# Where layer 1 of a graph network splits x into bf16 parts, and what its first product pass multiplies with

## The chip, the cores and the metric

One core of a Trainium2 chip runs the whole kernel in one launch. The metric is device microseconds of that core, first instruction to last; the median of several runs is quoted, and one execution was recorded by the hardware profiler. The core has five engines that run side by side: TensorE (PE in the profile; its weight loads are PEld), VectorE (DVE), ScalarE (ACT), GpSimd (POOL), and SyncE (SP), which here only issues DMA transfers.

## What is computed

Two SAGE layers on a graph of 12,500 nodes, 200,000 edges and 256 features, a dense layer, the residual and a layer norm. The reference, cut to its core:

```python
def _sage_conv(x, src, dst, W_l, b_l, W_r):
    msgs = x[src]
    agg = jax.ops.segment_sum(msgs, dst, num_segments=N_NODES)
    deg = jax.ops.segment_sum(jnp.ones((src.shape[0],), x.dtype), dst, num_segments=N_NODES)
    mean = agg / jnp.maximum(deg, 1.0)[:, None]
    return mean @ W_l + b_l + x @ W_r
...
h = jax.nn.relu(_sage_conv(x, src, dst, W1_l, b1, W1_r))
h = jax.nn.relu(_sage_conv(h, src, dst, W2_l, b2, W2_r))
return h @ W3 + b3
...
x = _layernorm(x + _L0_gnn_ref(x, edge_index, ...), axis=-1)
```

The edges come sorted by `dst`, and `dst` is 12500·u² of a uniform u, so that low nodes have very many edges.

## The kernel before

Nodes lie in blocks of 128 (98 blocks, the last one short). Each layer aggregates in two ways.

**Rounds (the cold nodes).** Nodes from 1536 up, in layer 1, get their neighbours by gathers. A round is four indirect DMAs on POOL (`gathered`, L266, issue on L273), each of 128 rows of 1 KB of x, into one of four `got` buffers; PE sums the rows by small products (`part_ps`, L285), ACT copies the sums out (L295), PE spreads them over nodes (`sum_ps`, L301, L307), and DVE adds them to a ring (L311, L315). Layer 1 has 257 rounds, layer 2 has 235. Finished blocks of nodes then go through `first_block` (L1055): x is loaded and transposed, PE multiplies with the weights (L1024, L1031), and h is written out as fp32 (L1075) and, split in three bf16 parts by `parts` (L689), as `h3_d` (L1078).

**Count products (the hot nodes).** The first 1536 nodes in layer 1 come in six groups of 256, taken in the order 5, 4, 3, 2, 1, 0. For a group, `count` (L803) builds a matrix of how many edges lead from each source node to each of the group's nodes: DVE makes comparisons (`pick` L821, `low` L824, `aft` L829), PE multiplies them (L859, L863), and ACT copies the counts into the bf16 matrix `counts` (L865). There are four `pick` buffers (L611). Then `product` (L725) multiplies x, block by block, with that matrix into `dense_ps`; `degrees` (L877) sums its columns.

A count is exact in bf16, but x is not: x is the exact sum of three bf16 parts (upper half of the fp32 bits, upper half of the rest, and what is then left). So a block's product is either 2 fp32 matmuls of 128x256 (the *plain* form, L765), for which ACT first widens the bf16 counts of two blocks to fp32 (`wide`, L762), or 6 bf16 matmuls of 128x256 on the three parts (L750), read back from `x3_d` in DRAM (L747, two blocks in one load of 384 KB). Which block takes which form stands in `stages_1` (L938):

- pass 1 (group 5): all 98 blocks plain; blocks 0 to 47 are also split here (`parts`: two DVE subtractions L694, L695 and two ACT copies L696, L697 for each block, 128x256) and written to `x3_d` (L771, 192 KB a block);
- pass 2 (group 4): blocks 0 to 47 from `x3_d`, blocks 48 to 97 plain, and split here;
- passes 3 to 6: all blocks from `x3_d`.

The split goes into three buffers `split3` (L600), which `first_block` uses for h too. x comes in pairs of blocks into the four `rows` buffers (L732, L736), three pairs ahead; `wide` has two buffers.

**What sets the order.** PE and POOL run in the order in which the program is written; the order on the others is made by the compiler from it. `layer` (L621) writes that order: before each round it spends a budget, `room_for` (5.3 for layer 1, L1119), in planned us for each of PE, DVE and ACT, with costs written out by hand (`ROUND`, `GROUP`, `DEGREE`, `COST_*` on L892 and L893, `count_cost`): first the round's own cost, then pieces of `first_block`, then *filler* until the fullest engine has its budget. The filler is `stages_1`: while one group is counted, the product of the group counted before is interleaved with it (`mixed`, L901), with the store of its counts (`stored`, L913) for layer 2. In the last 8 rounds whatever is left of the filler goes out at once. `freed` (L706) makes a load wait for the first gather product after those products that last used the buffer. SP issues all loads and stores but the gathers, in its order, each waiting in the queue for its data or its buffer.

Of the kernel before, what the change touches and what calls it, by code (L numbers as in the profile page):

```python
# [8 lines left out]
F32 = mybir.dt.float32  # L9
F32R = mybir.dt.float32r  # L10
F16 = mybir.dt.float16
BF16 = mybir.dt.bfloat16
# [3 lines left out]
OP = mybir.AluOpType  # L16
# [9 lines left out]
P = 128  # L26
# [23 lines left out]
def by_runs(  # L50
# [27 lines left out]
    nc = tc.nc  # L78
    N, D = x.shape
    E = src.shape[0]  # L80
    NB = -(-N // P)
    NC = D // P
# [23 lines left out]
    HG1, HG, DN = 6, 8, 256  # L106
# [7 lines left out]
    WIDEST = max(ROOMS)  # L114
# [18 lines left out]
    x3_d = dram.tile([P, NB, 3, D], BF16, name="x3_d")  # L133
# [183 lines left out]
    with tc.tile_pool(name="setup", bufs=1) as su, \  # L317
# [32 lines left out]
        whole = (NT // G) * G  # L350
        with nc.allow_non_contiguous_dma(reason="one edge of each tile"):
# [5 lines left out]
            if NT > whole:  # L357
                left = NT - whole
# [56 lines left out]
        first = su.tile([P, CH], F32, name="first")  # L415
# [55 lines left out]
        gathers_1 = Gathers(x, False)  # L471
# [20 lines left out]
        start = su.tile([P, HC], F32, name="start")  # L492
# [11 lines left out]
        for g in ORDER:  # L504
            c0, c1 = spans[g]
            n = c1 - c0
# [10 lines left out]
            of = off_f[:, lows[g]:highs[g]]  # L517
# [20 lines left out]
        for sign in (-1, 1):  # L538
            law = su.tile([1, NG], F32, name="law", bufs=2)
            for since, by in SLACKS:  # L540
                c = -(-since // G)
# [13 lines left out]
        for t in range(0, HT, 32):  # L555
            n = min(32, HT - t)
# [40 lines left out]
    keep = ctx.enter_context(tc.tile_pool(name="keep", bufs=1))  # L597

    SPLIT = 3
    split3 = keep.tile([P, SPLIT, 3, D], BF16, name="split")  # L600
# [3 lines left out]
    def held(g):  # L604

        return counts[ORDER.index(g) % 2]
# [1 line left out]
    NEAR = int(at_most(FIRST)) + room(FIRST - 1)  # L608
    assert NEAR <= DN

    picks = [keep.tile([P, WIDEST * NB], BF16, name=f"pick{i}") for i in range(4)]  # L611

    work = ctx.enter_context(tc.tile_pool(name="work", bufs=2))
    dense_pool = ctx.enter_context(tc.tile_pool(name="dense_ps", bufs=1, space=PSUM))
# [74 lines left out]
    def parts(t, s, rest):  # L689

        def upper(a):
            return a.bitcast(BF16).rearrange("p (n h) -> p n h", h=2)[:, :, 1]

        leaves = nc.vector.tensor_tensor(rest, t, upper(t), op=OP.subtract)  # L694
        nc.vector.tensor_tensor(s[:, 2], rest, upper(rest), op=OP.subtract)  # L695
        nc.scalar.copy(s[:, 0], upper(t))  # L696
        nc.scalar.copy(s[:, 1], upper(rest))  # L697
        return leaves
# [7 lines left out]
    def freed(load, n):  # L706

        if len(used) >= n and used[-n] < len(strips):
            tc.add_manual_dep(load.ins, strips[used[-n]], LANDED, reason="products done")

    N1 = 4
# [10 lines left out]
            freed(nc.sync.dma_start(counted, count_d[:, b:b + 2, pair:pair + 2]), STREAMS)  # L722
        return rows, counted

    def product(g, c_sb, plain=range(0), made=range(0)):  # L725


        ps = dense_pool.tile([P, NC, DN], F32, name="dense_ps")
        nc.tensor.matmul(ps, lhsT=zeros_b, rhs=c_sb[:, :NC, :DN], start=True, stop=False)
        own, wide = {}, {}  # L730

        def x_rows(u):  # L732
            t = rows_pool.tile([P, 2, 3, D], BF16, name="rows", bufs=N1)
            t = t.rearrange("p b k d -> p (b k d)").bitcast(F32)[:, :2 * D].rearrange("p (b d) -> p b d", d=D)
            n = min(2, (N - u * P) // P)
            freed(nc.sync.dma_start(t[:, :n], x[u * P:(u + n) * P].rearrange("(b p) f -> p b f", p=P)), 1)  # L736
            if n < 2:
                left = N - (u + n) * P
                nc.vector.memset(t[:, n], 0.0)
                nc.sync.dma_start(t[:left, n], x[(u + n) * P:N])  # L740
            return t

        for b in range(NB):
            if b not in plain:
                if b % 2 == 0:
                    rows = rows_pool.tile([P, 2, 3, D], BF16, name="rows", bufs=N1)
                    freed(nc.sync.dma_start(rows, x3_d[:, b:b + 2]), N1)  # L747
                for k in range(3):
                    for c in range(NC):
                        nc.tensor.matmul(ps[:, c], lhsT=rows[:, b % 2, k, c * P:(c + 1) * P],  # L750
                                         rhs=c_sb[:, b, :DN], start=False,
                                         stop=b == NB - 1 and k == 2 and c == NC - 1)
                cost = COST_1
            else:
                if b % 2 == 0:
                    for u in range(b, min(b + 2 * N1 - 2, plain[-1]), 2):
                        if u not in own:
                            own[u] = x_rows(u)
                    for u in range(b, min(b + 4, plain[-1]), 2):
                        if u not in wide:  # L760
                            wide[u] = rows_pool.tile([P, 2, DN], F32, name="wide", bufs=2)
                            nc.scalar.copy(wide[u], c_sb[:, u:u + 2, :DN])  # L762
                t, of = own[b - b % 2][:, b % 2], wide[b - b % 2]
                for c in range(NC):
                    nc.tensor.matmul(ps[:, c], lhsT=t[:, c * P:(c + 1) * P], rhs=of[:, b % 2],  # L765
                                     start=False, stop=b == NB - 1 and c == NC - 1)
                cost = COST_FIRST
                if b in made:
                    s = split3[:, b % SPLIT]
                    parts(t, s, work.tile([P, D], F32, name="rest", tag="own", bufs=3))  # L770
                    nc.sync.dma_start(x3_d[:, b], s)  # L771
                    cost = tuple(i + j for i, j in zip(cost, COST_SPLIT))
            if b % 2:
                used.append(len(strips))
            yield cost
        d_sb = rows_pool.tile([P, NC, DN], F32, name="d_sb", bufs=1)
        nc.scalar.copy(d_sb, ps)
        yield g, d_sb
# [98 lines left out]
    def degrees(g, c_sb):  # L877

        n0 = g * (DN // P)
        ps = dense_pool.tile([P, NC, DN], F32, name="dense_ps")  # L880
        for j in range(DN // P):
            for b in range(NB):
                nc.tensor.matmul(ps[:, 0, j:j + 1], lhsT=c_sb[:, b, j * P:(j + 1) * P], rhs=ones_b,
                                 start=b == 0, stop=b == NB - 1)
                if b % 14 == 13:
                    yield COST_DEGREES
        deg = work.tile([P, DN // P], F32, name="d_deg", bufs=1)
        nc.vector.tensor_scalar(deg, ps[:, 0, :DN // P], 1.0, None, op0=OP.max)
        nc.vector.reciprocal(rdeg[:, n0:n0 + DN // P], deg)


    COST_FIRST, COST_1, COST_2 = (0.92, 0.0, 0.31), (0.68, 0.0, 0.0), (0.7, 0.0, 0.0)  # L892
    COST_DEGREES, COST_SPLIT, COST_REST = (0.4, 0.0, 0.0), (0.0, 0.71, 0.81), (0.0, 0.0, 0.3)  # L893

    def count_cost(t):
        n = room(t) * NB
# [21 lines left out]
    def dense(waiting, made, with_deg=None):  # L918
        ready = []
        for p in made:  # L920
            if isinstance(p[0], float):
                yield p
            else:
                ready.append(p)
        if with_deg is not None:
            yield from degrees(with_deg, held(with_deg))
        for g, d_sb in ready:
            for j in range(DN // P):
                waiting.append((g * (DN // P) + j, d_sb[:, :, j * P:(j + 1) * P]))
# [4 lines left out]
    def counting(*gs):  # L934
        whole = sum(max(count_cost(t)) for g in gs for t in range(lows[g], highs[g]))
        return whole + NB // 14 * max(COST_REST) * len(gs)

    def stages_1(waiting):  # L938

        some = NB // 4 * 2  # L940
        for k, (g, last) in enumerate(zip(ORDER[:HG1] + [None], [None] + ORDER)):
            parts = [(count(g, held(g)), counting(g))] if g is not None else []
            if last is not None:
                plain = [range(0), range(NB), range(some, NB)][k] if k < 3 else range(0)
                made = [range(0), range(some), range(some, NB)][k] if k < 3 else range(0)
                whole = 5.0 + sum(max(COST_FIRST[e] * (b in plain) + COST_SPLIT[e] * (b in made) +
                                      COST_1[e] * (b not in plain) for e in range(3)) for b in range(NB))
                parts.append((dense(waiting, product(last, held(last), plain, made), last), whole))
                if last in SAVED:
                    parts.append((stored(last), MOVED))  # L950
            yield parts
# [25 lines left out]
    def staged(stages):  # L977
        def run(waiting):
            for parts in stages(waiting):
                yield from mixed(*parts)  # L980
        return run
# [134 lines left out]
    block_pool = None  # L1116
    with tc.tile_pool(name="count_ps", bufs=2, space=PSUM) as count_pool, \
            tc.tile_pool(name="rows_1", bufs=1) as rows_pool:
        layer(gathers_1, first_block, 3, staged(stages_1), 5.3, 8)  # L1119
    block_pool = ctx.enter_context(tc.tile_pool(name="block_ps", bufs=1, space=PSUM))  # L1120
    beside_pool = ctx.enter_context(tc.tile_pool(name="beside_ps", bufs=1, space=PSUM))
    count_pool = ctx.enter_context(tc.tile_pool(name="count_ps", bufs=1, space=PSUM))
    rows_pool = ctx.enter_context(tc.tile_pool(name="rows_2", bufs=1))
# [384 lines left out]
```

## Time and profile before

| | |
|---|---|
| median of 3 runs | 2687.47 us (2685.69 to 2693.3) |
| the profiled execution | 2681.34 us, its span 2679.5 us |
| mean granted PE clock in it | 0.968 of full speed |
| counting of group 5 ends, pass 1 begins | 181.7 us |
| passes 1 to 6 with their degrees end, about | 391.5, 599.5, 773.8, 960.8, 1252.9, 1401 us |
| last gather of layer 1, first of layer 2 | 1424.8, 1453.6 us |

Times are from the start of the span. Busy time is the time in which an engine ran an instruction; matmuls overlap one another, and their ends are modelled, so that a PE shown as busy is not PE at its peak. "PEclk" is the share of its full clock that TensorE was granted; "DMA share" is the mean busy share of the core's 16 DMA engines. In rows of groups, the numbers behind the bar are busy us and mean ns of one; then the engine's idle time just before them, and who ended it.

### The profile page before, as it was taken

To read this page: it belongs to the slowest core of one execution; us is meant where nothing else is said; L and a number is where in the kernel's file an instruction comes from. 1 tells how busy PE (TensorE), PEld (TensorE's weight loads), DVE (VectorE), ACT (ScalarE), POOL (GpSimd) and SP (SyncE) were. 2 spreads that over 40 slices of the span, in tenths; PEclk is the share of its full clock that TensorE was granted. 3 is DMA by queue.
4 is the path that set the end of the run, shared out by engine and by line. 5 is a ranking of instruction groups with operands and counts; after the bars stand their busy time and mean duration, and the time that the engine had idled before them with its cause. 6 is when DMAs were issued, how large, how long until landed. Compare 5 with 4: busy or idle time off the path is not lost. (4 is left out here: it accounts for less than half of the span.)

```text
span 2679.5 us, 51726 instructions
## 1 busy us (share of the span) xinstructions
PE 2411.8 (90%) x17119; PEld 1506.1 (56%) x17119; DVE 1558.3 (58%) x5514; ACT 1201.1 (45%) x2409; POOL 1910.2 (71%) x1978
## 2 busy tenths in 40 slices
PE   3678999889999999999997999999999999899986
PEld 2245676556776766666674445545455555555555
DVE  6777654775667789987334123544455554544455
ACT  0587764875667752386223012343434443222223
POOL 6767776776777777776664777777777777777772
PEclk8699999989999999999998999999999999999999
DMA  5359779889898777775875777778777777677653
GB/s 136 106 167 310 240 223 304 257 256 298 261 300 277 242 221 217 221 210 169 266 241 170 224 224 230 241 244 251 237 226 242 250 236 218 195 206 212 201 172 95
DMA packets 360737, 602.57 MB, mean 225 GB/s; under 512 B 56093, under 2 KB 244239, under 8 KB 360463
## 3 DMA queue, kind: packets, MB, share of 16 engines
q1 hardware_dynamic: 261637, 340.29, 39.8%
q0 software_dynamic: 94464, 258.08, 32.2%
q8 instruction: 141, 2.31, 0.4%
q10 hardware_dynamic: 4362, 0.80, 0.2%
q14 instruction: 133, 1.09, 0.1%
HBM read 509.09 MB, written 89.87 MB: 224 GB/s over the span
## 5 line engine op out<-in xcount | busy, mean ns | idle before, releaser
L273 POOL DMA_INDIRECT got<-in_x_dram,src_t x1028 | 1010.6, 983 | 412.3 <-issue 256.1
L273 POOL DMA_INDIRECT got<-h_d,src_t x940 | 897.3, 955 | 313.9 <-issue 251.4
L865 ACT CAST counts<-count_ps 128x882 f32 (+3 forms) x688 | 620.4, 902 | 232.7 <-PE count_ps L859 185.0
L859 PE MATMUL count_ps<-pick,low 128*128 128x490 bf16 (+2 forms) x1188 | 350.8, 350 | 56.9 <-ACT counts L865 44.9
L750 PE MATMUL dense_ps<-counts,rows 128*128 128x256 bf16 x2640 | 359.3, 276 | 23.3 <-DMA rows<-x_d 22.5
L285 PE MATMUL part_ps<-got,one 128*32 128x257 f32 (+1 forms) x3936 | 325.3, 403 | 58.7 <-DMA got<-h_d,src_t 34.8
L790 PEld LDWEIGHTS <-rows 128*128 128x128 bf16 x2352 | 214.0, 97 | 259.4 <-issue 81.4
L821 DVE TENSOR_SCALAR pick<-steps,tables 128x686 bf16<-128x686 f16 (+3 forms) x816 | 335.1, 411 | 24.7 <-PE count_ps L863 11.7
L295 ACT COPY some<-part_ps 128x257 f32<-128x257 f32 (+1 forms) x349 | 130.0, 373 | 472.5 <-PE part_ps L285 467.4
L750 PEld LDWEIGHTS <-rows 128*128 128x128 bf16 x2640 | 241.7, 98 | 104.8 <-issue 33.2
L229 DVE TENSOR_TENSOR one<-lo_t,lane_b 128x128 f32<-128x128 bf16 x492 | 140.7, 287 | 233.5 <-PE part_ps L285 232.3
L824 DVE TENSOR_SCALAR low<-lanes,low_t 128x130 bf16<-128x130 f16 x816 | 220.8, 272 | 82.5 <-PE count_ps L863 78.3
L315 DVE TENSOR_TENSOR sums<-sums,sum_ps 128x256 f32 x349 | 143.0, 410 | 154.6 <-PE sum_ps L301 134.8
L301 PE MATMUL sum_ps<-two,some 128*128 128x128 f32 x1396 | 222.6, 283 | 9.7 <-ACT own_t L997 7.6
L301 PEld LDWEIGHTS sum_ps<-two,some 128*128 128x128 f32 x1396 | 202.7, 195 | 41.4 <-ACT own_t L997 12.9
L790 PE MATMUL beside_ps<-counts,rows 128*128 128x512 bf16 x588 | 224.5, 382 | 0.5 <-ACT split L800 0.5
L790 PE MATMUL dense_ps<-counts,rows 128*128 128x512 bf16 x588 | 224.6, 382 | 0.0
L1038 DVE TENSOR_TENSOR own<-block_ps,biases 128x256 f32<-128x256 f32 x196 | 83.0, 424 | 216.9 <-PE block_ps L1031 214.5
L859 PEld LDWEIGHTS <-low 128*128 128x128 bf16 x1188 | 114.7, 99 | 150.4 <-issue 38.2
L285 PEld LDWEIGHTS part_ps<-got,one 128*32 128x32 f32 x3936 | 80.2, 109 | 202.5 <-issue 162.0
L997 ACT COPY own_t<-block_ps 128x256 f32<-128x256 f32 x294 | 105.4, 373 | 168.0 <-PE block_ps L995 164.8
L1034 ACT COPY sums<-zero 128x256 f32<-128x256 f32 x168 | 67.7, 403 | 240.9 <-PE block_ps L1031 240.9
(197 smaller groups left out, 3588.2 us busy)
## 6 DMA issues: line engine op xcount, KB each, us to landing
rows<-x_d SPq DMA_DIRECT2D x220, 384.0 KB
rows<-h_d SPq DMA_DIRECT2D x196, 384.0 KB
count_d<-counts SPq DMA_DIRECT2D x28, 896.0 KB
x_sb<-in_x_dram SPq DMA_DIRECT2D x194, 128.0 KB
h_d<-split SPq DMA_DIRECT2D x98, 192.0 KB
x_d<-split SPq DMA_DIRECT2D x98, 192.0 KB
rows<-in_x_dram SPq DMA_DIRECT2D x72, 256.0 KB
got<-in_x_dram,src_t POOLq DMA_INDIRECT x1028
```

What stands on the lines that cost most here:

```text
L229: nc.vector.tensor_tensor(one, lo[:, a:a + n * (G - 1) + 1:n].unsqueeze(2).to_broadcast([P, G, W]), lane_b[:, :W].unsqueeze(1).to_broadcas ...
L273: rows = nc.gpsimd.indirect_dma_start(out=g[:, j, :D], out_offset=None, in_=self.table, in_offset=bass.IndirectOffsetOnAxis(ap=src_t[:, e: ...
L285: strip = nc.tensor.matmul(part_ps[j * W:(j + 1) * W, :width], lhsT=one[:, j], rhs=g[:, j, :width], start=r == 0, stop=r == n - 1)
L295: nc.scalar.copy(some[:, :width], part_ps[:, :width])
L301: nc.tensor.matmul(sum_ps[:, c], lhsT=some[:, c * P:(c + 1) * P], rhs=two, start=True, stop=True)
L315: adds.append(nc.vector.tensor_add(own, own, sum_ps[:, :NC]).ins)
L750: nc.tensor.matmul(ps[:, c], lhsT=rows[:, b % 2, k, c * P:(c + 1) * P], rhs=c_sb[:, b, :DN], start=False, stop=b == NB - 1 and k == 2 and ...
L790: nc.tensor.matmul(ps[c], lhsT=rows[:, b % 2, k, c * P:(c + 1) * P], rhs=counted[:, b % 2], start=b + k == 0, stop=b == NB - 1 and k == 2)
L821: nc.vector.tensor_scalar(r[:, :w * NB], steps[:, :w * NB], key_t[g][:, t - lo_g:t - lo_g + 1], None, op0=OP.is_equal)
L824: nc.vector.tensor_scalar(low.rearrange("p (a b) -> p a b", a=5), lanes_5[:, :, :LW // 5], low_t[:, t:t + 1], None, op0=OP.is_equal)
L859: nc.tensor.matmul(c[:, a * NB:b * NB], lhsT=s, rhs=r[:, a * NB:b * NB], start=True, stop=alone)
L865: nc.scalar.copy(to[:, :, bass.ds(off_act.at(t), w)], c.rearrange("p (d s) -> p s d", s=NB))
```

## The change

Pass 1 now splits all 98 blocks and multiplies the parts at once; passes 2 to 6 all read `x3_d`. x comes in pairs into two tiles of its own, `x_pair`; `parts_of` splits a pair (128x512) with two subtractions on DVE and two copies on ACT straight into a `rows` tile, which pass 1's bf16 products read and which one store of 384 KB writes to `x3_d`. Loads of x are asked for two pairs ahead and splits one pair ahead. The fp32 products, the widened counts and the use of `split3` for x are gone, and there are three `pick` buffers for four (in both layers). The planned cost of a pass-1 block is 0.68 on PE, 0.61 on DVE and 0.70 on ACT, and layer 1's budget for a round is 5.05 for 5.3. Layer 2's text is otherwise the same.

```diff
-    picks = [keep.tile([P, WIDEST * NB], BF16, name=f"pick{i}") for i in range(4)]
+    picks = [keep.tile([P, WIDEST * NB], BF16, name=f"pick{i}") for i in range(3)]
...
+    def parts_of(t, s):
+        def upper(a):
+            return a.bitcast(BF16).rearrange("p b (n h) -> p b n h", h=2)[:, :, :, 1]
+        rest = rows_pool.tile([P, 2, D], F32, name="rest_2", bufs=1)
+        nc.vector.tensor_tensor(rest, t, upper(t), op=OP.subtract)
+        freed(nc.vector.tensor_tensor(s[:, :, 2], rest, upper(rest), op=OP.subtract), N1)
+        freed(nc.scalar.copy(s[:, :, 0], upper(t)), N1)
+        nc.scalar.copy(s[:, :, 1], upper(rest))
+
+    def x_rows(u):
+        t = rows_pool.tile([P, 2, D], F32, name="x_pair", bufs=2)
+        n = min(2, (N - u * P) // P)
+        nc.sync.dma_start(t[:, :n], x[u * P:(u + n) * P].rearrange("(b p) f -> p b f", p=P))
...
+    def product(g, c_sb, first=False):
         ps = dense_pool.tile([P, NC, DN], F32, name="dense_ps")
         nc.tensor.matmul(ps, lhsT=zeros_b, rhs=c_sb[:, :NC, :DN], start=True, stop=False)
+        raw, made = {}, {}
         for b in range(NB):
+            if b % 2 == 0 and first:
+                for u in range(b, min(b + 6, NB), 2):
+                    if u not in raw:
+                        raw[u] = x_rows(u)
+                for u in range(b, min(b + 4, NB), 2):
+                    if u not in made:
+                        made[u] = rows_pool.tile([P, 2, 3, D], BF16, name="rows", bufs=N1)
+                        parts_of(raw[u], made[u])
+                        nc.sync.dma_start(x3_d[:, u:u + 2], made[u])
+                rows = made[b]
+            elif b % 2 == 0:
+                rows = rows_pool.tile([P, 2, 3, D], BF16, name="rows", bufs=N1)
+                freed(nc.sync.dma_start(rows, x3_d[:, b:b + 2]), N1)
+            for k in range(3):
                 for c in range(NC):
+                    nc.tensor.matmul(ps[:, c], lhsT=rows[:, b % 2, k, c * P:(c + 1) * P],
+                                     rhs=c_sb[:, b, :DN], start=False,
+                                     stop=b == NB - 1 and k == 2 and c == NC - 1)
...
+            yield COST_FIRST if first else COST_1
...
-    COST_FIRST, COST_1, COST_2 = (0.92, 0.0, 0.31), (0.68, 0.0, 0.0), (0.7, 0.0, 0.0)
-    COST_DEGREES, COST_SPLIT, COST_REST = (0.4, 0.0, 0.0), (0.0, 0.71, 0.81), (0.0, 0.0, 0.3)
+    COST_FIRST, COST_1, COST_2 = (0.68, 0.61, 0.7), (0.68, 0.0, 0.0), (0.7, 0.0, 0.0)
+    COST_DEGREES, COST_REST = (0.4, 0.0, 0.0), (0.0, 0.0, 0.3)
...
-        layer(gathers_1, first_block, 3, staged(stages_1), 5.3, 8)
+        layer(gathers_1, first_block, 3, staged(stages_1), 5.05, 8)
```

More of the change, by code (lines that the diff above doesn't have):

```diff
@@ L723, in loaded @@
         return rows, counted
-    def product(g, c_sb, plain=range(0), made=range(0)):
+    def parts_of(t, s):
[6 more added lines that the diff above has]
+        nc.scalar.copy(s[:, :, 1], upper(rest))
@@ L728, in product @@
+    def x_rows(u):
+        t = rows_pool.tile([P, 2, D], F32, name="x_pair", bufs=2)
+        n = min(2, (N - u * P) // P)
+        nc.sync.dma_start(t[:, :n], x[u * P:(u + n) * P].rearrange("(b p) f -> p b f", p=P))
+        if n < 2:
+            left = N - (u + n) * P
+            nc.vector.memset(t[:, n], 0.0)
+            nc.sync.dma_start(t[:left, n], x[(u + n) * P:N])
+        return t
+    def product(g, c_sb, first=False):
         ps = dense_pool.tile([P, NC, DN], F32, name="dense_ps")
@@ L729, in product @@
         nc.tensor.matmul(ps, lhsT=zeros_b, rhs=c_sb[:, :NC, :DN], start=True, stop=False)
[L730 to L741, printed above, removed]
@@ L743, in product @@
-        for b in range(NB):
[L744 to L763, printed above, removed]
-                for c in range(NC):
[L765 to L772, printed above, removed]
@@ L773, in product @@
             if b % 2:
                 used.append(len(strips))
-            yield cost
+            yield COST_FIRST if first else COST_1
         d_sb = rows_pool.tile([P, NC, DN], F32, name="d_sb", bufs=1)
@@ L938, in stages_1 @@
     def stages_1(waiting):
-        some = NB // 4 * 2
         for k, (g, last) in enumerate(zip(ORDER[:HG1] + [None], [None] + ORDER)):
@@ L943, in stages_1 @@
             if last is not None:
[L944 to L948, printed above, removed]
+                whole = 5.0 + NB * max(COST_FIRST if k == 1 else COST_1)
+                parts.append((dense(waiting, product(last, held(last), k == 1), last), whole))
                 if last in SAVED:
```

## The prediction

> **What bounds the kernel now.** I read the groups first, then the windows of the six passes, then who waits. The edit is in layer 1, which is a race between PE and POOL's gathers.
>
> ```profile
> L273 POOL DMA_INDIRECT got<-in_x_dram,src_t x1028 | 1010.6, 983 | 412.3 <-issue 256.1 <-PE part_ps L285 119.0 <-DMA got<-in_x_dram,src_t 10.9
> ...
> L821 DVE TENSOR_SCALAR pick<-steps,tables 128x686 bf16<-128x686 f16 (+3 forms) x816 | 335.1, 411 | 24.7 <-PE count_ps L863 11.7 <-PE count_ps L859 9.7 <-PE count_ps L848 0.9
> ```
>
> Layer 1's 1028 gathers take 1010.6 us on POOL, and 256.1 us pass between them without a wait: (1010.6+256.1)/1028 = 1.232 us each, 4.93 us for a round of four. That is POOL's floor. Of the rest 119.0 us are waits for PE. (L821 makes the picks; I use it below.)
>
> Windows cut where each pass ends (count behind POOL: gathers issued):
>
> ```profile
> 181.70:391.50 209.80, 192.84 (x1339) 131.69 (x1339) 135.70 (x492) 152.75 (x298) 153.14 (x156) 0.97 0.84 261
> 391.50:599.50 208.00, 185.11 (x1443) 125.60 (x1440) 137.21 (x504) 136.46 (x294) 146.46 (x147) 0.93 0.86 272
> 599.50:773.80 174.30, 168.62 (x1537) 120.09 (x1535) 111.88 (x428) 109.99 (x179) 121.30 (x127) 0.95 0.85 278
> 773.80:960.80 187.00, 181.40 (x1632) 129.14 (x1631) 137.78 (x552) 131.68 (x235) 134.03 (x139) 0.99 0.84 269
> 960.80:1252.90 292.10, 276.39 (x2204) 184.52 (x2205) 265.95 (x992) 151.24 (x319) 213.28 (x220) 0.98 0.69 205
> 1252.90:1401.00 148.10, 139.90 (x1276) 103.93 (x1276) 56.54 (x193) 40.68 (x111) 97.08 (x103) 0.98 0.79 255
> sum 1219.30, PE 1144.26 PEld 794.97 DVE 845.07 ACT 722.80 POOL 865.29; mean PE 190.71 PEld 132.50 DVE 140.84 ACT 120.47 POOL 144.21
> ```
>
> The gathers give 39, 37, 32, 35, 55 and 26 rounds, 223 in all: 1219.3/223 = 5.47 us a round, above POOL's floor and above the planned 5.3. PE is busy in 1144.26 of 1219.30 us and idle in 75.0. So PE sets most of the pace, with POOL 10% behind it. Passes 1 and 2, which the change touches, have 17.0 and 22.9 us of idle PE; pass 3, already pure bf16, has 5.7.
>
> **The change, part by part.**
>
> *fp32 products out, bf16 products in.* The timeline of PE, one block in each form, with the next instruction behind it:
>
> ```profile
> 242.02 1.13 PE L765 MATMUL dense_ps<-wide,rows 128*128 128x256 f32 x4
> 242.99 0.37 PE L859 MATMUL count_ps<-pick,low 128*128 128x490 bf16 x1
> ```
> ```profile
> 399.82 0.61 PE L301 MATMUL sum_ps<-two,some 128*128 128x128 f32 x4
> ...
> 400.51 0.38 PE L859 MATMUL count_ps<-pick,low 128*128 128x490 bf16 x1
> ...
> 401.60 0.64 PE L285 MATMUL part_ps<-got,one 128*32 128x257 f32 x8
> 402.17 0.83 PE L750 MATMUL dense_ps<-counts,rows 128*128 128x256 bf16 x6
> 402.84 0.37 PE L859 MATMUL count_ps<-pick,low 128*128 128x490 bf16 x1
> ```
>
> From start to start a plain block takes 0.97 us (2 matmuls, 4 instructions in the trace), a bf16 block 0.67. The difference is 0.30 us. Plain blocks are 98 in pass 1 and 50 in pass 2: 148 x 0.30 = **44.4 us** less PE work, 29.4 and 15.0.
>
> *ACT and DVE.*
>
> ```profile
> L765 PE MATMUL dense_ps<-wide,rows 128*128 128x256 f32 x592 | 160.2, 396 | 5.6 <-ACT wide L762 5.6
> L229 DVE TENSOR_TENSOR one<-lo_t,lane_b 128x128 f32<-128x128 bf16 x492 | 140.7, 287 | 233.5 <-PE part_ps L285 232.3
> L695 DVE TENSOR_TENSOR split<-rest 128x256 bf16<-128x256 f32 x196 | 80.6, 416 | 38.0 <-DMA x_d<-split 33.9 <-DMA h_d<-split 3.4
> L762 ACT CAST wide<-counts 128x512 f32<-128x512 bf16 x74 | 45.6, 618 | 0.2 <-PE dense_ps L765 0.2
> L694 DVE TENSOR_TENSOR rest<-rows 128x256 f32<-128x256 f32 x98 | 40.0, 416 | 6.3 <-DMA h_d<-own 3.4 <-ACT split L697 2.7
> L696 ACT COPY split<-rows 128x256 bf16<-128x256 bf16 x98 | 39.6, 405 | 37.2 <-DMA x_d<-split 28.5 <-DMA h_d<-split 4.3 <-issue 2.9
> ```
>
> The 592 instructions are the 148 plain blocks. A 128x512 subtraction isn't in the trace. From 287 ns at 128 wide and 416 at 256 it goes on to 416+258 = 674; twice 416 = 832 is the upper end. I take 0.67. A copy at 512 is between 0.41 and 0.81 (one and two of 405); the widening, also 512 wide, took 0.618, which I take. DVE in pass 1: 48 blocks x 0.832 = 39.9 out, 49 pairs x 2 x 0.67 = 65.7 in, so 135.7 becomes about 161. ACT in pass 1: 49 widenings (30.3) and 48 x 0.81 (38.9) out, 60.6 in: about 144. In pass 2 50 blocks x 0.832 (DVE), 50 x 0.81 and 25 x 0.618 (ACT) go, and nothing comes: 41.6 and 56.0 us. None of this is on the path as a sum; it counts by the waits:
>
> ```profile
> PE count_ps L859 <- ACT counts L865: 9.4, 10, 2.8
> PE dense_ps L750 <- DMA rows<-x_d: 5.9, 3, 3.1
> PE dense_ps L883 <- ACT d_sb L777: 5.4, 1, 5.4
> ```
>
> These are PE's longest waits in pass 2. Two are for an ACT that falls from 136 to 80 us of work there. Pass 3 has no such wait in its list. I count **10 us** won of 14.8; the load stays late. In pass 1 PE's waits for `wide` (5.6 us in the L765 row) and ACT's and DVE's for the stores out of three `split3` buffers (28.5 and 33.9, both stages) go. Parts take their place as what PE waits for: a chain of two where there was one copy. I call that even.
>
> *The plan.* Budget and costs are in the code; adding them up as `layer` does gives 39, 36, 32, 34, 55, 26 rounds to the passes before (the trace agrees to a round) and 35, 31, 33, 37, 59, 26 after. The total hardly moves, and each round's own PE work goes with it. So PE's total simply falls by 44.4. But pass 1 now has little PE work: 192.8-29.4-4x1.2 = 158.6 us (1.2: a round's strips, from 401.60 to 402.17, and its spreading, from 399.82 to 400.51, rounded down since not every round spreads). POOL's floor there is 35 x 4.93 = 172.6. With its own waits for PE (13.7 us before), pass 1 takes 186 us, with 27 us of idle PE against 17: **10.4 us** of the saving are lost. Pass 5 has 59 rounds, floor 291; with 281 of PE work and the old 16 idle it takes 297, so POOL doesn't decide there.
>
> *DMA.* Pass 1 moved this:
>
> ```profile
> DMA packets 45462, 54.80 MB, mean 261 GB/s; under 512 B 4590, under 2 KB 40026, under 8 KB 45439
> ```
> ```profile
> 200.00:220.00 20.00, 16.75 (x104) 10.32 (x103) 14.30 (x55) 14.38 (x32) 14.98 (x16) 0.91 1.09 368
> 420.00:440.00 20.00, 14.86 (x99) 9.17 (x97) 5.86 (x22) 6.08 (x10) 7.82 (x9) 0.74 0.87 288
> ```
>
> The stores of 50 more blocks add 9.8 MB, four rounds fewer take 2.1: 62.5 MB. At the 368 GB/s of the fullest window that is 170 us, at pass 1's own ratio (261 GB/s at share 0.84, so 311) 201. The first hides behind 186, the second doesn't; I take 186, since the present split phase ran at 368, and keep 15 us for the range. SP issues 49 fewer stores and 25 more loads of `x3_d`.
>
> *Three picks.* A `pick` waits for the product two steps back instead of three. The 816 picks of both layers now wait 24.7 us in all (the L821 row), nearly all on PE's products. One buffer fewer can't gain; if the waits double and half of that passes on to PE, it costs 12 us. I take 3, near the low end, since a DVE that waits for PE holds nothing up unless DVE is full, as in pass 5 only (265.95 of 292.10).
>
> *Sum:* -44.4 -10 +10.4 +3 = **-41 us**. Layer 2 keeps its text (but for the picks) and its time. The profiled execution took 2681.34, so 2640; the median of the runs was 6.1 higher, so **2646**.
>
> **The rivals.**
>
> *POOL paces (R1).* PE's busy time overlaps its own pipeline. [...] In the rows: POOL's 119.0 us of waits for PE over layer 1 are 119.0/257 = 0.46 us a round, so in the 66 rounds that passes 1 and 2 keep 30 us could be won at most; less the 10.4 of new idle time that is 20, or 2667. The step of 0.67 against 0.97 us speaks for my forecast. For this one speaks a window late in pass 1, where PE shows no idle time at all and POOL still issues 17 gathers in 20 us, its full pace:
>
> ```profile
> 340.00:360.00 20.00, 20.00 (x126) 13.92 (x125) 10.55 (x40) 13.64 (x23) 15.13 (x17) 1.00 0.61 180
> ```
>
> *The floor is reached (R2).* If rounds get as near to their 5.05 as pass 5's came to 5.3, 221 rounds x 5.07 = 1120 instead of 1219; less the 223 x 0.17 = 38 us by which rounds now exceed their 5.3, about 60 us won: 2628.
>
> *Pass 1 starves on x (R3, slower).* x has two tiles, and SP issues a pair's load behind the store of the pair two before, which waits for its parts. So a pair takes (load + split)/2. Pass 1 lasts 49 x that, plus 10 for degrees. How long a load takes when the queues are full:
>
> ```profile
> 417.58 0.45 SPq L747 DMA_DIRECT2D rows<-x_d  x1
> ```
> ```profile
> 419.55 0.82 PE L750 MATMUL dense_ps<-counts,rows 128*128 128x256 bf16 x6
> ...
> 423.52 0.83 PE L750 MATMUL dense_ps<-counts,rows 128*128 128x256 bf16 x6 [3.15 <-DMA rows<-x_d]
> ...
> 425.52 1.49 PE L750 MATMUL dense_ps<-counts,rows 128*128 128x256 bf16 x6
> ```
>
> 5.9 us for 384 KB. With 256 KB at 5 and a split of 2 us the pair takes 3.5: no harm. With a load of 7, behind a 384 KB store in the same queue, and a split of 3.5, it is 5.25: pass 1 lasts 267 us, 81 more than forecast, and the time is 2727. The kernel is slower from 4.5 us a pair on (10+49x4.5 = 231, 45 over the forecast). PE's clock adds to it: after the 3.15 us stall six matmuls took 1.49 us for 0.83, at a granted 0.74. [...] Against the rival: DVE and ACT have room in pass 1, and POOL hides the first 172 us.
>
> *Nothing (R4):* the saving goes into new waits for parts; 2687.
>
> **How the numbers follow.** Forecast 45%, with its own range 2630 to 2662; R1 18%, R2 14%, R3 16%, R4 7%. A measurement tells about 0.3% (8 us) from no change. Faster: forecast, R1 and R2, 0.77; the same 0.07; slower 0.16. The range takes in R1, R2, R4 and the 15 and 12 us of the open prices, and leaves out most of R3 and the lowest end of R2: 2610 to 2700.
>
> **What would show it.** Right: pass 1 near 186 us, pass 2 near 170, passes 3 to 6 within 10 of before; no fp32 rows in `dense_ps`; pairs split in 0.67 and 0.62 us; POOL's waits for PE down to some 80 us. Wrong: PE waiting for `rows` with x loads behind it in pass 1 and a clock under 0.9 (R3); POOL at 1.24 us a gather all through with PE idle (R1); DVE waiting for L859 at the picks in pass 5 (their price). What I can't see is the order that the compiler gives DVE, ACT and SP for the new text.

## The result, and the profile after

The kernel after takes **2660.14 us** (median of 4 runs, 2652.59 to 2667.07), the kernel before 2686.58 on the same chip: a ratio of 0.9897 (95% 0.9864 to 0.993), 26 us faster where 41 were forecast, and inside the forecast's own range of 2630 to 2662. The profiled execution is the slowest of the four: 2667.07 us, with a span of 2665.2.

The windows of the six passes, in the columns of the prediction's table (length, busy us of PE, PEld, DVE, ACT and POOL, granted clock, DMA share, GB/s):

```profile
196.80:391.40 194.60, 168.60 (x1486) 112.62 (x1485) 149.25 (x471) 143.03 (x238) 149.10 (x135) 0.95 0.94 304
391.40:556.50 165.10, 156.90 (x1459) 111.79 (x1458) 101.08 (x377) 92.48 (x153) 124.86 (x130) 0.95 0.89 286
556.50:735.50 179.00, 169.60 (x1563) 121.88 (x1561) 114.75 (x437) 112.20 (x185) 128.44 (x134) 0.98 0.85 272
735.50:930.00 194.50, 187.98 (x1672) 131.55 (x1668) 138.83 (x558) 135.82 (x240) 144.61 (x149) 0.97 0.84 269
930.00:1228.60 298.60, 281.13 (x2254) 186.19 (x2254) 271.27 (x1008) 149.05 (x325) 227.90 (x233) 0.99 0.69 207
1228.60:1375.60 147.00, 140.13 (x1292) 105.15 (x1290) 58.87 (x201) 42.94 (x117) 106.61 (x111) 0.99 0.84 268
sum 1178.80, PE 1104.33 PEld 769.17 DVE 834.04 ACT 675.52 POOL 881.50; mean PE 184.05 PEld 128.19 DVE 139.01 ACT 112.59 POOL 146.92
```

The passes take 1178.8 us for 1219.3, **40.5 less**, with 39.9 us less PE work, idle PE as before (74.5 for 75.0), and the same gathers in them (888 in one window over all six; a sum over the six rows gives 892, since a gather that straddles an edge counts twice): 5.29 us a round for 5.47, by the prediction's 223 rounds. But the table begins at 196.80, not 181.70. The whole account of the profiled span is therefore: 15.1 us later into pass 1, 40.5 less in the passes, 5.6 more from pass 6's end to layer 2's first gather (1433.8), 5.5 more in layer 2; together 14.3 less. (196.80 is the weight load ahead of pass 1's first product, 181.70 that product itself, whose weight load came at 180.7; on like footing pass 1 begins 16.1 us later.) The medians are 12 us further apart than these two executions.

The groups of the new split and product (busy us and mean ns of one behind the bar, then the engine's idle time before them and who ended it):

```profile
L770 PE MATMUL dense_ps<-counts,rows 128*128 128x256 bf16 x3528 | 482.7, 275 | 34.9 <-DMA rows<-x_d 24.7 <-ACT rows L734 5.8 <-ACT rows L735 4.4
...
L732 DVE TENSOR_TENSOR rest<-x_pair 128x512 f32<-128x512 f32 x49 | 33.6, 686 | 42.1 <-DMA x_pair<-in_x_dram 39.9 <-ACT rows L735 0.8 <-ACT counts L865 0.5
L733 DVE TENSOR_TENSOR rows<-rest 128x512 bf16<-128x512 f32 x49 | 33.3, 680 | 0.0
...
L734 ACT COPY rows<-x_pair 128x512 bf16<-128x512 bf16 x49 | 30.4, 619 | 28.0 <-DMA x_pair<-in_x_dram 24.8 <-DMA x_d<-rows 3.2
L735 ACT COPY rows<-rest 128x512 bf16<-128x512 bf16 x49 | 30.3, 619 | 8.4 <-DVE rest L732 8.3
```

No fp32 product is left in `dense_ps`: 3528 is 6 passes x 98 blocks x 6. The pairs' four instructions come at the forecast's durations. DVE's 39.9 us of waits for x fall in two places: 22.6 in pass 1 and 17.3 in one piece, at the very start. There the timelines of DVE, SP and POOL show what the passes don't:

```profile
8.56 0.68 DVE L410 CAST src_f<-src_i 128x1152 f32<-128x1152 int32 x1
26.51 0.69 DVE L732 TENSOR_TENSOR rest<-x_pair 128x512 f32<-128x512 f32 x1 [17.27 <-DMA x_pair<-in_x_dram]
27.23 0.69 DVE L733 TENSOR_TENSOR rows<-rest 128x512 bf16<-128x512 f32 x1
27.84 1.54 DVE L404 TENSOR_SCALAR src_t<-src_ps 128x512 int32<-128x512 f32 x3
```
```profile
23.68 3.95 SPq L741 DMA_DIRECT2D x_pair<-in_x_dram  x3
```
```profile
28.80 1.63 POOL L273 DMA_INDIRECT got<-in_x_dram,src_t  x1 [25.93 <-DVE src_t L404]
```

Read them upward. POOL's first gather needs the index table `src_t` that DVE makes at L404. DVE has done L410 at 9.2 us, but the next instruction in its queue is pair 0's first subtraction, whose x SP asks for only at 23.68, behind the loads of the edge lists and of `x_sb`. So DVE stands still for 17.27 us and takes nothing from behind the waiting instruction, though for most of that time work there was ready: by 11.3 us PE had made what the first L404 reads. Before, the first gather was issued at this time:

```profile
11.42 1.10 POOL L273 DMA_INDIRECT got<-in_x_dram,src_t  x1 [8.55 <-DVE src_t L404]
```

The compiled order of DVE says the same without any time (line, operation; four neighbouring entries):

```
L410 TensorCopy src_f<-src_i
L732 TensorTensor rest<-x_pair
L733 TensorTensor rows<-rest
L404 TensorScalarPtr src_t<-src_ps x3
```

The split's operands are all free from the start (`x_pair` and `rows` are used by nobody before), so nothing kept the compiler from putting it ahead of the tables. Before, x was first split at 179.0 us (in the row below the shortest, median and longest ns stand ahead of the comma, the first and last start behind it), in buffers that it shared with h; that the sharing held it back is argued, not tried.

```profile
L694 DVE TENSOR_TENSOR rest<-rows x98: 361/416/482, 179.0 to 589.1; 128x256 f32<-128x256 f32 x98
```

What POOL waits for in layer 1, after:

```profile
POOL got L273 <- issue: 263.6, 863, 0.6
POOL got L273 <- PE part_ps L285: 44.9, 43, 7.7
POOL got L273 <- DVE src_t L404: 25.9, 1, 25.9
```

The waits for PE fall from 119.0 to 44.9 us, where the forecast had some 80; the third row is the start (8.5 us before).

### The profile page after: what moved, and what is told of

Read it like the earlier page. It is cut to its first block, busy times and chain, and to the rows that moved or that the text cites. A ratio compares the mean times of both kernels' runs of the same rounds, so it can differ in the third digit from the quotient of the medians.

```text
span 2665.2 us, 51823 instructions
## 1 busy us (share of the span) xinstructions
PE 2374.8 (89%) x17415; PEld 1482.8 (56%) x17415; DVE 1553.7 (58%) x5415; ACT 1157.3 (43%) x2237; POOL 1929.9 (72%) x1978
## 4 chain that ended last, share of the span: by engine, by line
PE 59%; DMA 14%; POOL 8%; DVE 7%; issue 6%; ACT 3%; DVEq 0%; ACTq 0%; SPq 0%; POOLq 0%
PE dense_ps L770 11%; POOL got L273 8%; PE part_ps L285 7%; PE count_ps L859 6%; PE block_ps L1020 6%; PE beside_ps L790 5%; PE dense_ps L790 5%; PE block_ps L1027 5%; DMA got<-h_d,src_t 5%; PE sum_ps L301 4%; DMA rows<-x_d 4%; PE block_ps L1096 3%; DMA x_pair<-in_x_dram 2%; ACT counts L865 2%; DMA x_sb<-in_x_dram 2%
## 5 line engine op out<-in xcount | busy, mean ns | idle before, releaser
L273 POOL DMA_INDIRECT got<-in_x_dram,src_t x1028 | 1026.8, 999 | 371.8 <-issue 263.6
L770 PE MATMUL dense_ps<-counts,rows 128*128 128x256 bf16 x3528 | 482.7, 275 | 34.9 <-DMA rows<-x_d 24.7
L770 PEld LDWEIGHTS <-rows 128*128 128x128 bf16 x3528 | 322.5, 98 | 148.6 <-issue 46.3
L790 PEld LDWEIGHTS <-rows 128*128 128x128 bf16 x2352 | 214.4, 98 | 259.8 <-issue 83.0
L821 DVE TENSOR_SCALAR pick<-steps,tables 128x686 bf16<-128x686 f16 (+3 forms) x816 | 333.8, 413 | 27.1 <-PE count_ps L859 15.1
```

The costliest lines, as they stand in the source:

```text
L273: rows = nc.gpsimd.indirect_dma_start(out=g[:, j, :D], out_offset=None, in_=self.table, in_offset=bass.IndirectOffsetOnAxis(ap=src_t[:, e: ...
L790: nc.tensor.matmul(ps[c], lhsT=rows[:, b % 2, k, c * P:(c + 1) * P], rhs=counted[:, b % 2], start=b + k == 0, stop=b == NB - 1 and k == 2)
L821: nc.vector.tensor_scalar(r[:, :w * NB], steps[:, :w * NB], key_t[g][:, t - lo_g:t - lo_g + 1], None, op0=OP.is_equal)
```

## The experiments

Theory: the form and its plan win what the forecast summed, and the 17 us of late gathers give part of it back. Rivals: the smaller budget, or three picks, make the difference; x starves pass 1; PE isn't what paces. Four kernels ran beside the kernel before on one chip (2689.80 us there, 29 runs), called the first chip below. That it is the chip of the result is likely by the times and not on record.

**e1_tables_first.** `later` orders an instruction behind the tables of the first gathers; the program has it already.

```diff
-        nc.vector.tensor_tensor(rest, t, upper(t), op=OP.subtract)
+        later(nc.vector.tensor_tensor(rest, t, upper(t), op=OP.subtract))
```

> The change, with one order added: the first subtraction of a split may not stand ahead of the tables of the first gathers on DVE. Theory: in the changed kernel DVE's order has pair 0's split ahead of the tables, DVE waits 17 us for that pair's load, and the first gather starts at 28.8 us instead of 11.4. So here the first gather starts near 11 us, pass 1 near 182, the six passes stay at 1179 us, and the time falls from 2660 by 15 to 17, to about 2644, which is the 41 us that were forecast. Rival: the late start is the chance of one execution, or it is made up later; then the time stays at 2660 within 5.

Measured: 2647.16 us (2640.54 to 2655.24), ratio 0.9858 (0.983 to 0.9885): **42.6 us faster than before**, the fastest version measured. Its first gather on POOL's timeline, and its windows (pass 1 and the sum of the six):

```profile
11.42 1.11 POOL L273 DMA_INDIRECT got<-in_x_dram,src_t  x1 [8.54 <-DVE src_t L404]
```
```profile
191.30:380.60 189.30, 166.88 (x1486) 111.71 (x1485) 147.84 (x469) 143.33 (x238) 145.92 (x135) 0.96 0.96 312
...
sum 1168.10, PE 1096.43 PEld 764.07 DVE 832.57 ACT 675.15 POOL 881.59; mean PE 182.74 PEld 127.34 DVE 138.76 ACT 112.53 POOL 146.93
```

The gathers begin at 11.42 again, as expected. The two stages did not come as expected: pass 1 begins at 191.3, not near 182, and the passes take 1168.1 us, not 1179, which is 51.2 less than before's. On medians the hoisted instruction cost 13 us, on another chip (f1 against f0, below) 11. The two ratios' intervals overlap in both pairs, so the cost in time is likely and not shown; that the gathers start 17.4 us late, and that this one order dependency ends it, is plain in the traces.

**e3_old_form_new_budget.** Before, with the budget of after.

```diff
-        layer(gathers_1, first_block, 3, staged(stages_1), 5.3, 8)
+        layer(gathers_1, first_block, 3, staged(stages_1), 5.05, 8)
```

> The kernel before with the budget of 5.05 us a round and nothing else. Theory (PE's work sets the six passes, the budget only has to fit it): PE's work is what it was, so the six passes take about 1219 us again, spread over more rounds, with some 50 us of products left for the last 8 rounds, when POOL has nothing to do; 2687, within 12. Rival (the budget is what brings the gain, since rounds were planned longer than POOL's floor): 2660 or less.

Measured: 2682.36, ratio 0.9985 (0.9966 to 1.0005), no difference that can be told. Its passes in one window, and POOL's waits for PE in layer 1:

```profile
187.70:1402.70 1215.00, 1141.52 (x9412) 795.33 (x9411) 837.36 (x3155) 714.92 (x1432) 868.32 (x888) 0.97 0.80 253
```
```profile
POOL got L273 <- PE part_ps L285: 96.4, 28, 60.1
```

The passes take 4 us less and end where they did, with 125 gathers ahead of pass 1 for 122. The budget alone wins 9 us at most (the interval's lower end). POOL's waits tell more: but for one of 60.1 us, when the leftover products run ahead of the last gathers, they come to 36.3 us for the 119.0 of before. So POOL's waits in the rounds can go without any gain in time; what is then left over on PE is waited for at the end.

**e4_new_form_old_budget.** After, with 5.3.

```diff
-        layer(gathers_1, first_block, 3, staged(stages_1), 5.05, 8)
+        layer(gathers_1, first_block, 3, staged(stages_1), 5.3, 8)
```

> The change with the old budget of 5.3 us a round. Theory: the filler is used up some 17 rounds early, and these rounds run at POOL's floor of 4.93 us with PE half idle. 17 rounds of 4.93 are 84 us, in place of 17 rounds' own PE work of 1.2 to 1.5 us each, 25, that leaves the passes: up to 59 us worse than the change, so 2700 to 2719. Rival (the gain is the form's alone): 2660 within 8.

Measured: 2705.59, ratio 1.0058 (1.0037 to 1.0078), **slower than before**. The windows of its passes, and of what is left of layer 1's gathers:

```profile
196.60:1344.60 1148.00, 1069.21 (x9404) 745.53 (x9403) 801.50 (x2936) 654.15 (x1190) 810.27 (x823) 0.97 0.80 258
1344.60:1452.40 107.80, 84.15 (x481) 56.68 (x481) 50.62 (x180) 34.88 (x105) 81.80 (x86) 0.79 0.60 180
```
```profile
POOL got L273 <- PE part_ps L285: 117.1, 99, 6.8
```

The passes end 31 us earlier than after's, but 86 gathers are left over, with no filler to lie beside: 107.8 us for them, 1.25 each, POOL's own pace. The last gather comes at 1452.4 (before 1424.8). POOL's waits for PE in layer 1 (the last row) are as long as before the change, with the new form: they follow the budget. With too large a budget a round gets more filler than it can hide, and the cold nodes' rounds are left alone at the end.

**e5_three_picks.** Before, with three `pick` buffers.

```diff
-    picks = [keep.tile([P, WIDEST * NB], BF16, name=f"pick{i}") for i in range(4)]
+    picks = [keep.tile([P, WIDEST * NB], BF16, name=f"pick{i}") for i in range(3)]
```

> The kernel before with three pick buffers for four. Theory: 0 to 5 us slower (the forecast took 3), since PE's waits for picks grew from 1.4 and 1.1 us to 4.5 and 1.6 in the changed kernel. Rival: 12 us slower, the upper end, with part of it in layer 2, where the changed kernel's profiled execution was 5 us slower than before.

Measured: 2690.33, ratio 1.0004 (0.9986 to 1.0022): between 4 us won and 6 lost.

**The other eight ran on other chips**, where the kernel before itself takes about 3185 us (e2, e6, e8 on one, the f runs on a second) and 3147 (g, later, on a chip that the record gives the same number as e2's). Their times stand against those alone. First the change and e1 again, unedited:

> The change as it is, beside the next three kernels on one chip. On a chip where the kernel before takes about 2688, 2660 within 8. If the chip is again one where the kernel before takes 3185, this run says whether the change itself loses there (the three-tile version took 1.0054 of the kernel before): by the theory, which has the gain in PE's work, it can only lose if something other than PE's work paces layer 1 there.

> The tables-first version once more, to be compared with the change on the same chip: 13 to 17 us below it (theory), 0 to 5 (rival: the late start is chance).

Measured: 3221.56 for the change, ratio 1.0118 (1.0064 to 1.0173), and 3210.49 with the tables first, 1.008 (1.0039 to 1.012). The same two kernels that win 26 and 43 us on the first chip lose 36 and 25 here. The 11 us between them lie between what was expected and the rival. The change's six passes in one window, three rows of POOL's waits in layer 1, and the chain's engines:

```profile
225.30:1680.00 1454.70, 1204.69 (x9708) 809.69 (x9707) 834.90 (x3048) 665.48 (x1255) 877.14 (x888) 0.90 0.67 212
```
```profile
POOL got L273 <- issue: 245.2, 799, 0.6
POOL got L273 <- PE part_ps L285: 218.3, 74, 10.5
POOL got L273 <- remote: 61.4, 41, 2.9
```
```profile
PE 61%; issue 8%; another core or an unknown queue 8%; DVE 5%; ACT 4%; DMA 2%; DVEq 0%; SPq 0%; ACTq 0%
```

The passes take 276 us more than on the first chip with PE busy in 83% of them (94% there), at a clock of 0.90 for 0.97. The third row, "remote", names a releaser that the profile can't place; the first chip's list has no such row. The last fence is the chain that ended last, by engine: 8% of this span is another core or an unknown queue, so again a releaser that the profile can't place.

**g_before_more_pe.** Before, with three more products by zeros in each of the 148 plain blocks. They add zero to the sums and some 49 us of PE work (444 x 0.11, a sixth of a bf16 block's 0.67; in the trace three of them take 0.33 us from start to start).

```diff
             for b in ...
+                for _ in range(3):
+                    nc.tensor.matmul(ps[:, 0], lhsT=zeros_b, rhs=c_sb[:, b, :DN], start=False, stop=False)
```

> The kernel before with three more bf16 matmuls of 128x256 (zeros as weights, so that they add nothing) in each of its 148 plain blocks: 148 x 0.33 = 49 us more PE work in passes 1 and 2, the opposite of what the change takes away there, with nothing else touched. On a chip where the kernel before takes about 2688: theory (PE paces the passes, as the forecast had it), passes 1 and 2 together grow by 38 to 49 us, to 2726 to 2737; the forecast's first rival (POOL paces, PE's busy time overstates), 20 or less, 2708 or below. On a chip where it takes about 3185, where more PE work in pass 1 of the changed kernel cost nothing: under 15 us, and the trace stands in for one of the kernel before there, to be laid beside that of the change.

Measured: 3140.46 against 3147.19, ratio 0.9987 (0.9959 to 1.0015). The sum of its passes:

```profile
sum 1418.50, PE 1238.84 PEld 849.89 DVE 849.58 ACT 722.10 POOL 862.94; mean PE 206.47 PEld 141.65 DVE 141.60 ACT 120.35 POOL 143.82
```

49 us of PE work in the old passes 1 and 2 cost at most 5 us there (the interval's upper end). On such a chip PE doesn't pace these two passes, so a change that takes 44 us of PE work out of them has nothing to win by that there. Laid beside the change's (f0, on the other slow chip), the old form with these products takes 478.0 us for 428.2 in passes 1 and 2, and 940.5 for 1026.5 in passes 3 to 6, where f0 has 39 more gathers. So rounds move from the first two passes to the later ones there too, and the later ones grow by more than the first two shrink. Which part of the change does it is open: layer 2 takes 0.9% longer in f0 (1481.9 us for 1468.3) and the six passes 2.6%, so the chips' difference is hardly all of it, and no run there has the new budget or the new form alone.

**e6_more_pe and f6_more_pe.** e1 with the same three products in each of pass 1's 98 blocks (294 x 0.11 = 32 us).

```diff
             for k in range(3):
                 for c in range(NC):
                     ...
+            if first:
+                for _ in range(3):
+                    nc.tensor.matmul(ps[:, 0], lhsT=zeros_b, rhs=c_sb[:, b, :DN], start=False, stop=False)
```

> The tables-first version with three more bf16 matmuls of 128x256 (with zeros as weights, so that they add nothing) in each of pass 1's 98 blocks: 98 x 0.33 = 32 us of PE work given back where the change took 29. Theory (pass 1 has some 20 us of idle PE, which the forecast put at 27, so a third to a half of the work is hidden): pass 1 grows by 12 to 22 us, the time to 2659 to 2669. Rival 1 (PE sets pass 1 fully): 32 us, 2679. Rival 2 (POOL or DMA set it alone): under 5 us, 2647 to 2652.

> 32 us of PE work more in pass 1 (98 x 3 matmuls with zeros), on top of the tables-first version, against it on the same chip: 12 to 22 us more (theory: a third to a half is hidden), 32 (rival: PE sets pass 1 fully), under 5 (rival: POOL or DMA alone).

Measured: 3208.85, ratio 1.0044 (1.0015 to 1.0072), and 3200.84, 1.0055 (1.0019 to 1.009); f6 is no slower than f1, which is the last rival's case. Pass 1 of f6, then of f1:

```profile
226.00:454.60 228.60, 206.43 (x1779) 143.26 (x1778) 150.93 (x465) 143.32 (x238) 149.88 (x142) 0.93 0.83 265
```
```profile
218.10:444.40 226.30, 182.55 (x1485) 117.16 (x1484) 149.73 (x469) 143.28 (x238) 156.85 (x142) 0.90 0.84 268
```

PE is busy 23.9 us longer, the pass lasts 2.3 longer. On that chip PE doesn't pace pass 1. Whether it does on the first chip is not answered by this.

**e2_three_x_tiles, f2_three_x_tiles and e8_one_x_tile.** e1 with three tiles for x (and two `split3` buffers, to make room), and with one.

```diff
-        t = rows_pool.tile([P, 2, D], F32, name="x_pair", bufs=2)
+        t = rows_pool.tile([P, 2, D], F32, name="x_pair", bufs=3)
...
-    SPLIT = 3
+    SPLIT = 2
```
```diff
-        t = rows_pool.tile([P, 2, D], F32, name="x_pair", bufs=2)
+        t = rows_pool.tile([P, 2, D], F32, name="x_pair", bufs=1)
```

> The tables-first version with three tiles for x instead of two (and two split buffers for h instead of three, to make room). Theory: pass 1 is held by POOL's floor (35 rounds x 4.93 = 173 us) and by a DMA that is 0.96 busy, and only a little by the two tiles; DVE's 23 us of waits for x pairs go, pass 1 falls from 189 us by 0 to 8, the time from 2647 to 2639 to 2647. Rival (the third rival of the forecast in a mild form, the x stream sets pass 1): pass 1 falls to 175 or less, the time to 2633 or less.

> Three tiles for x on top of the tables-first version, against it on the same chip: 0 to 8 us less (theory: POOL's floor and the DMA hold pass 1), 14 or more less (rival: the x stream does).

> The tables-first version with one tile for x instead of two, so that a pair's load waits for the split of the pair before. It measures the price in the forecast's slower rival. By that rival's formula a pair takes load + split, 5 + 2 us, and pass 1 lasts 49 x 7 + 10 = 353 us instead of 189: 2811. If the load is shorter than the 5 us assumed (3 us), 49 x 5 + 10 = 255: 2713. Were the load hidden, it would stay within 10 us of 2647.

Measured: 3201.33, ratio 1.0054 (1.0027 to 1.0081); 3199.56, 1.0074 (1.0042 to 1.0105); 3215.56, 1.0089 (1.0063 to 1.0116). Pass 1 with three tiles (e2), then with one (e8, on the same chip):

```profile
218.10:442.70 224.60, 186.10 (x1485) 118.41 (x1484) 149.32 (x464) 142.90 (x237) 150.97 (x142) 0.89 0.84 269
```
```profile
223.90:462.60 238.70, 185.84 (x1483) 112.31 (x1482) 152.87 (x470) 148.78 (x240) 146.68 (x142) 0.92 0.79 255
```

In pass 1 a third tile wins nothing over two (225.9 in f2, 226.3 in f1); f2's median is 11 us below f1's, but their ratios' intervals nearly coincide. With a single tile a pair's load and split can't overlap the next one's, and pass 1 still takes only 14.1 us more: (238.7-10)/49 = 4.7 us a pair is the most that load and split take together there, on average, so 2.3 with two tiles.

## Why the prediction was right in direction and too large by 15 us

- **PE's term, 44.4 us: right.** PE's work in the passes fell by 39.9, and by 47.8 in e1; the passes shortened by 40.5 and 51.2. A bf16 block still goes from start to start in 0.65 to 0.67 us. In the five kernels whose passes are shown at this speed (before, after, e1, e3, e4) PE's busy time in the passes runs from 1069.2 to 1144.3 us, and each time the passes last 72 to 79 us longer than it: their length goes by PE's work. No run there adds work to PE alone.
- **Pass 2's waits, 10 us won: right, a little small.** Idle PE there went from 22.9 to 8.2, pass 2 took 165.1 for 170. The wait for ACT's counts is gone from PE's list, the load stays, as forecast:

```profile
PE dense_ps L770 <- DMA rows<-x_d: 6.6, 5, 4.9
PE dense_ps L883 <- ACT d_sb L777: 1.0, 1, 1.0
```

- **Pass 1's new idle time, 10.4 us: right (9.0).** Pass 1 took 194.6 for 186, and 189.3 in e1: its idle time is as forecast, but PE's work in it is 168.6 for 158.6. The other passes took most of that back; over all six PE's work is 4.5 us above the forecast. PE waits there for parts, counts and gathers alike:

```profile
PE part_ps L285 <- DMA got<-in_x_dram,src_t: 6.1, 3, 2.7
PE dense_ps L770 <- ACT rows L734: 5.8, 3, 3.9
PE count_ps L859 <- ACT counts L865: 5.3, 4, 2.3
PE dense_ps L770 <- ACT rows L735: 4.4, 8, 1.1
```

  Pass 1 moved 59.18 MB (forecast 62.5 MB) at 304 GB/s and a share of 0.94. Scaled to a full share as the prediction does, that is 323 GB/s, between the 311 and 368 from which the 15 us of doubt were worked out; the 304 itself is below both.
- **Three picks, +3: nothing that can be told** (e5).
- **Rounds:** 34, 33, 34, 37, 58 and 28 for 35, 31, 33, 37, 59 and 26; passes 3 to 6 within 8 us of before.
- **R1 (POOL paces, 2667):** nearest to the measured time, by luck and not by its mechanism. It allowed 30 us from POOL's waits for PE in the two passes; those waits fell by 74 us in layer 1 and the passes by 40.5. That they fell is the budget's doing: with the budget alone they go too, but for one at the end, and nothing is won (e3), and with the old budget they stay (e4). PE's busy time does overlap (six products of a block are busy for 0.82 us in after, and the next instruction starts 0.65 us behind their start), yet for how long the passes last it was a good guide at this speed: 72 to 79 us less than they take, in all five kernels. The weight loads fill 65% of the passes in each of the five (64.9 to 65.5) and tell them apart no better. POOL fills 73% of pass 1 in before (153.14 of 209.8 us), as does ACT; with the gaps between its gathers taken as busy, 39 rounds of 4.93 us, it would be 92%. POOL isn't far: its gathers with their gaps now take (1026.8+263.6)/1028 = 1.255 us, 5.02 a round, against 5.29 measured; its busy time is this row:

```profile
L273 POOL DMA_INDIRECT got<-in_x_dram,src_t x1028 | 1026.8, 999 | 371.8 <-issue 263.6
```

- **R3 (x starves pass 1):** DVE does wait for x there, 22.6 us, but no 4.5 us a pair come of it: (189.3-10)/49 is 3.7 in e1. On the other chip e8 bounds load and split together at 4.7 us, where the rival's bad case took 10.5. PE's clock in pass 1 was 0.95, not under 0.9.

```profile
DVE rest L732 <- DMA x_pair<-in_x_dram: 22.6, 16, 6.9
```

- **What failed is what the sum left out.** It began at pass 1 and took layer 2's time as unchanged. Inside the passes the profiled execution won 40.5 us, as summed; it lost 15.1 ahead of them, 5.6 behind them and 5.5 in layer 2. The forecast said that it couldn't see the order that the compiler gives DVE, and gave that no price. The order put one split ahead of the first gathers' tables, and e1, which changes only that, lands at -42.6 for a forecast of -41. That agreement is in part luck: in e1's profiled execution the passes won 10 us more than summed, and 9.6 went ahead of pass 1 and 5.6 in layer 2.
- **How the 15.1 us split up isn't settled.** Pass 1's first weight load comes at 180.7 us in before, 177.3 in e5, 187.7 in e3 and 191.3 in e1, all without the late start, and at 196.6 in e4 and 196.8 in after, both with it. Of these, after and e1 differ in the order alone: 5.5 us. By e3 the budget takes 7 us, by e4 against after nothing; and the rest of the order's 13 us shows later, in single executions.

Not settled: what paces pass 1 on the first chip (PE, DVE's x or the DMA queues at a share of 0.94 to 0.96), since e6 and e2 didn't run there; whether the 5.5 us each of layer 2 in after and e1 are more than spread (with three picks it took 1228.9 in e5 and 1226.8 in e4, with four 1225.9 in before and 1222.5 in e3: an order that would fit a price of the picks, which e5's interval puts at 6 us at most); and why the change loses on the other chips, where it is shown only that PE doesn't pace the first two passes.

## What to carry to other kernels

When a change gives a piece of work its own buffers, it may also lose the waits that kept it in its place: look through the compiled order of each engine for the new instructions' first places, and price what stands behind them (here the first gather, at 28.80 us for 11.42). A plan with a budget and the form it was made for belong together: here the budget alone moved nothing that can be told, the form with the old budget was slower than before, both together won 1.0%, and with one order dependency 1.4%. Waits that go away are no measure of what was won: POOL's waits for PE fell with the budget alone (119.0 to 96.4 us), and the time didn't (ratio 0.9985, 0.9966 to 1.0005). A saving in one engine's work is worth its full size only where that engine paces, and that can differ between two chips with the same kernel: with 39.9 us less PE work the passes were 40.5 us shorter in the result; 49 us of PE work added to two passes cost at most 5 us on a slow chip.

## What the runs showed of the hardware

One waiting instruction held DVE for 17.27 us with ready work behind it, and so the gathers (the first at 28.80 us for 11.42). The kernel before took 2687 to 2690 us on one chip and 3147 to 3185 on others. The change ran at a mean granted clock of 0.97 on the first and 0.915 on another, with waits there ("remote", 61.4 us of POOL's in layer 1) that the first chip doesn't show. On one of the slow chips 444 more products in the kernel before, 49 us of PE work, made no difference in the time that can be told (ratio 0.9987, 0.9959 to 1.0015).
